# Four row blocks instead of six in the first phase of a two-layer graph kernel, a seven-product output projection, and an earlier place for a row of scores

## The chip, the cores and the metric

The kernel runs on one core of one Trainium2 chip. The metric is the device time of one execution in microseconds (us), lower is better. The time before is a median of three runs. A profile of one more execution shows what each engine did: TensorE (PE; its weight loads are listed as PEld), VectorE (DVE), ScalarE (ACT), GpSimd (POOL) and SyncE (SP, which only issues DMAs here).

## The reference

Two layers over a sparse graph with N = 4096 nodes and F = 512 features, all in fp32. `adj` is 4096 x 4096, some 0.8% of it nonzero, symmetric in its pattern. Cut to what is computed:

```python
h = relu(layernorm(x))                        # layer 0
d = rowsum(adj) ** -0.5
x = x + relu((d[:, None] * adj * d[None, :]) @ h @ W0 + b0)

h = relu(layernorm(x))                        # layer 1, attention
Wh1, Wh2 = h @ W1 @ a[:F], h @ W1 @ a[F:]
e = leaky_relu(Wh1 + Wh2.T, 0.2)
att = softmax(where(adj > 0, e, -1e12), axis=1)
neg = -softmax(where(adj > 0, -e, -1e12), axis=1)
x = x + elu(concat([att @ h, neg @ h], axis=1) @ wtrans)
```

Layer 0 multiplies by all of `adj`; layer 1 needs only the rows of `h` at the nonzero places of `adj`.

## The kernel before, in words

The nodes are cut into 32 blocks of 128 rows, called tiles here. A matmul of two fp32 operands appears in the profile as two records, and each has its own weight load. [...] an accumulator holds its bank from its first matmul until another engine has read it.

**First phase.** A loop over the 32 row blocks j loads x[j] (POOL's queue), normalizes and transposes it (`turn_x`), projects it with W0 (`project`, L679), and loads the four quarters of adj[j] (SP's queue, nine buffers) whose sums on ACT and DVE give d[j]. `scale` (L702) evicts the projection as y0[j]. In the same loop the tiles of the first entry of `GROUPS`, six of them (26 to 31), are accumulated directly: `load_at` fetches the block of the transposed adjacency `adj_t` (SP's queue, five buffers), `multiply` (L852) does one product of 128 x 512 per tile into one bank each, and `pack` turns the block into a mask of bytes (DVE here) and writes it to tables in DRAM on POOL's queue.

**Groups.** The other 26 tiles go in seven groups, the rest of `GROUPS`: six of four tiles and, last, (24, 2). The function `group` walks over 16 pairs of row blocks jp. Two tiles times two row blocks are a 2 x 2 block product, which is done by seven products of 128 x 256 instead of eight (`multiply_blocks`, L893). It uses sums of blocks of `adj_t` (`sum_at`, L880 to L883, DVE, three buffers named sums) and sums of y0 (`sum_y`, made in the first such group). A tile of `at` covers 8 // n row blocks, so one load, and one set of sums, serves one jp in a group of four and two jps in a group of two. While a group multiplies, the group before it is finished: `join_blocks` (or `evict` for the first phase's accumulators) combines the products on DVE, and `finish0` adds bias and residual, normalizes into h on ACT (two buffers h), computes two dot products with h on DVE (L816), writes x1, and puts h in eight tables, one copy on POOL's queue and seven on ACT's. In each step `finish0` of one tile is called. `EARLY` names groups whose masks are made early, by the index b of the group in which that happens. From b = 3 and b = 5 on, lists of the nonzero places are made on DVE, piece by piece in each step (`listing`, L391 and L393), and joined by POOL's DMAs.

**Between the layers.** In the last group gathering for layer 1 starts. The memory is cut into pools that are stacked from the left, and others from the right: `late_mask` and `late` (late_h, ut0, s_pair) lie on the right. A pool that lies over an earlier one waits for the last reader of that memory.

**Layer 1.** `sparse_layer1` handles half tiles r of 64 rows, two to a tile, in the order `order`; the tile of `PAIR0` was done ahead. For each tile POOL issues 22 indirect gathers of 128 rows (L451) in three parts into six buffers; even r use the first two parts, odd r the last two. `weights` makes scores (L463), leaky relu (L469), both exponentials (ACT, L473), masks (L482), and sums by a tree (L487 to L493), two half tiles ahead of the product. `product` does 14 accumulating products (L1296, 28 records), a matmul `cs` for the sums, and an eviction with the inverse sums on ACT (L1305). `turn` transposes the result into ut on PE and ACT (L508, L512). After each odd r but the first, `finish1` does the output projection of a tile by eight products of 128 x 512 (L1319, 16 records) with wtrans in memory as wt_sb, applies elu and adds x1 (L1327 to L1331), and writes the tile. The rows of Wh1, the scores s, come by `load_s` (L1256) on SP's queue, in four-tile pieces.

The order on each engine is fixed when the program is built. The builder places instructions by its own estimate of when they are ready, starting from the order in the source; `tc.keep_in_program_order` exempts some. Once built, each engine works through its own list in order, and a wait holds up what stands behind it.

Of the kernel before, what the change touches and what calls it, by code (L numbers as in the profile page):

```python
# [20 lines left out]
IB = 512  # L21


GROUPS = ((26, 6), (16, 4), (20, 4), (0, 4), (4, 4), (8, 4), (12, 4), (24, 2))

EARLY = {(24, 2): (2,), (12, 4): (3,), (8, 4): (4,)}
PAIR0 = 16
Y_PARTS = (8, 11, 13)
T_PARTS = (7, 9)
# [230 lines left out]
def gcn_gat_kernel(  # L260
# [251 lines left out]
            nc.scalar.copy(ut[:, g, :, (r % 2) * RB : (r % 2 + 1) * RB], tp[:, :, g, :])  # L512


    late_mask = ctx.enter_context(sbuf(name="late_mask", bufs=1, side="right"))
    late_m = late_mask.tile([P, EJ, TT * P], U8, name="late_m")
    with sbuf(name="y0", bufs=1) as y_pool, sbuf(name="wa", bufs=1) as wa_pool, sbuf(name="bits", bufs=4) as bits_pool, sbuf(name="small0", bufs=4) as small, ExitStack() as rest, ExitStack() as lists:
        list_pool = lists.enter_context(sbuf(name="list", bufs=1, side="right"))
# [232 lines left out]
            nc.vector.scalar_tensor_tensor(y, acc, d_all[:, j : j + 1], b_bc, ALU.mult, ALU.add)  # L751
            return y

        def new_y(work, j, k):
            if k < 0:
                return work.tile([P, F], F32, tag="y", name=f"y{j}", bufs=4)
            if k == 0:
                spare.append(make_pool.tile([P, 3, F], F32, tag="keys", name="spare"))
            return spare[0][:, k]

        def evict(i0, acc, work, _):

            return {
                i0 + k: affine(new_y(work, i0 + k, k - 3), a, i0 + k) for k, a in enumerate(acc)
            }

        def join_blocks(i0, n, acc, work, new_w):

            ys = {}
            for x in range(n // 2):  # L770
                p16, p23, p45, p7 = acc[x]
                j0, j1 = i0 + x, i0 + n // 2 + x
                ys[j0], ys[j1] = y, v = [new_y(work, j, -1) for j in (j0, j1)]
                w = new_w(f"w{j0}")[:, :H]
                nc.vector.tensor_copy(y[:, :H], p16[:, :H])
                nc.vector.tensor_tensor(w, p16[:, H:], y[:, :H], ALU.add)  # L776
                nc.vector.tensor_tensor(y[:, H:], p45[:, H:], w, ALU.add)

                def first(p23=p23, y=y):
                    nc.vector.tensor_tensor(y, p23, y, ALU.add)  # L780

                def second(p7=p7, w=w, p45=p45, v=v):
                    two = "p (a f) -> p a f"
                    nc.vector.tensor_tensor(w, p7, w, ALU.add)
                    nc.vector.tensor_tensor(
                        v.rearrange(two, a=2),
                        p45.rearrange(two, a=2),
                        w.unsqueeze(1).to_broadcast([P, 2, H]),
                        ALU.add,
                    )  # L790
# [12 lines left out]
            return ys  # L803
# [178 lines left out]
                pack(bits6, i0, j, ats.pop(j), j < 2)  # L982
                mark()
        pending = (GROUPS[0], partial(evict, i0, acc))
        listing, joining, spare = [], [], []

        def make_lists(g):
            make_keys(g)
# [43 lines left out]
        def group(b, work, at_pool, sum_pool, step, prod, n_h=2):  # L1032

            nonlocal pending
            i0, n = GROUPS[b]
            nj = 8 // n
            (p0, pn), take = pending
            order = [p0 + k for k in ((0, 2, 1, 3) if b > 1 else range(pn))]
            ats, sums = {}, {}

            def prepare(jp):
                if 2 * jp % nj == 0:
                    ats[jp] = load_at(at_pool, i0, n, 2 * jp, nj)
                    sums[jp] = sum_at(sum_pool, ats[jp], n, f"sums{i0}_{jp}")
                else:
                    ats[jp], sums[jp] = ats[jp - 1], sums[jp - 1]
                if b == 1:
                    sum_y(jp)

            prepare(0)  # L1050
            for j in order[:2]:
                if j not in xrs:
                    load_xr(j)
            for jp in range(NP):
                if jp + 1 < NP:
                    prepare(jp + 1)
                mark()
                if jp == 0:
                    ys = take(work, prod)
                    p7 = bank(f"p7_{i0}")  # L1060
                    acc = [
                        [*(bank(f"p{k}_{i0 + x}") for k in (16, 23, 45)), p7[:, x * H : (x + 1) * H]]
                        for x in range(n // 2)
                    ]
                multiply_blocks(acc, n, jp, ats[jp], sums[jp])
                if (i0, n) not in EARLY:
                    pack(bits_pool, i0, 2 * jp, ats[jp])
# [23 lines left out]
        with sbuf(name="work0", bufs=2) as work, sbuf(name="sums", bufs=3) as sum_pool, sbuf(name="at", bufs=6) as at_pool:  # L1091

            def prod(name):
                return work.tile([P, F], F32, tag="q", name=name, bufs=1)

            for b in range(1, len(GROUPS) - 1):

                def step(jp):
                    if jp == 2 and b in (3, 5):
                        make_lists((1, 0)[b == 5])  # L1100
                    for _ in range((2, 3)[b == 6] if jp != 2 else 0):
                        if listing:
# [10 lines left out]
        late = ctx.enter_context(sbuf(name="late", bufs=1, side="right"))  # L1113
# [122 lines left out]
    def sparse_layer1():  # L1236
        with ExitStack() as pools:
# [5 lines left out]
            slots = ((0, 0), (1, 0), (1, 2), (1, 1), (0, 1), (0, 2))  # L1243
            g_pools = {s: pool("g%d%d" % s, 1) for s in slots}
            tmp, small, p_pool = pool("tmp", 1), pool("small1", 2), pool("p", 3)
            work, ut_pool, wt_pool = pool("work1", 2), pool("ut", 2), pool("wt", 1)
            warm = small.tile([P, 1], F32, tag="warm", name="warm", bufs=1)
            nc.scalar.activation(warm, sign, AF.Exp)
            wt_sb = wt_pool.tile([P, 2 * FC, F], F32, name="wt_sb")
            s_pool = pool("s", 2)  # L1250
            gath, wgt, us, uts, srow = {}, {}, {}, {PAIR0: ut0}, {}

            def load_s(k):

# [52 lines left out]
            def turn(r):  # L1307
                if r % 2 == 0:
                    uts[r // 2] = ut_pool.tile([P, 2, FC, P], F32, tag="ut", name=f"ut{r // 2}")
                turn_u(r, us.pop(r), uts[r // 2])  # L1310

            def finish1(j):
                ut = uts.pop(j)
                x1 = work.tile([P, F], F32, tag="x1", name=f"x1_{j}")
                nc.sync.dma_start(out=x1, in_=x1_dram[j])
                po = bank(f"o1_{j}")
                for g in range(2):
                    for c in range(FC):
# [4 lines left out]
                            start=g == 0 and c == 0,  # L1323
                            stop=g == 1 and c == FC - 1,
                        )
                e = work.tile([P, F], F32, tag="eo", name=f"eo{j}", bufs=1)
                nc.vector.tensor_scalar(e, po, 0.0, None, ALU.min)  # L1327
                nc.scalar.activation(e, e, AF.Exp)
                y = work.tile([P, F], F32, tag="y", name=f"y1_{j}", bufs=1)
                nc.vector.scalar_tensor_tensor(y, po, 0.0, x1, ALU.max, ALU.add)  # L1330
                nc.vector.scalar_tensor_tensor(e, e, -1.0, y, ALU.add, ALU.add)  # L1331
                nc.sync.dma_start(out=out[j * P : (j + 1) * P, :], in_=e)


            pairs = [(PAIR0 + n) % (NR // 2) for n in range(1, NR // 2)]
# [24 lines left out]
            for k, r in enumerate(order):  # L1360
# [8 lines left out]
                if k + 2 < len(order):  # L1369
                    weights(order[k + 2])  # L1370
                    if wanted and order[k + 2] % 8 == 7:
                        load_s(wanted.pop(0))
                if k:
                    turn(order[k - 1])
                if k == 2:
                    finish1(PAIR0)
                if k % 2 and k > 1:
                    finish1(order[k - 3] // 2)
            turn(order[-1])
            finish1(order[-1] // 2)  # L1380

# [41 lines left out]
```

## Time and profile before

| | us |
|---|---|
| runs | 2130.96, 2139.83, 2135.72 |
| median of the runs | 2135.72 |
| the profiled execution | 2098.72 |
| its span, first to last instruction | 2096.8 |
| PE busy | 1996.2 |
| DVE busy | 1120.1 |
| POOL busy | 917.0 |
| ACT busy | 511.3 |
| granted TensorE clock, mean | 0.981 |

The stages of the profiled execution, by PE's matmuls:

| stage | us from the span's start |
|---|---|
| first phase, L852 | 25.8 to 334.5 |
| group (16, 4) | 334.3 to 433.5 |
| group (20, 4) | 433.4 to 530.7 |
| group (0, 4) | 530.6 to 638.1 |
| group (4, 4) | 637.9 to 753.6 |
| group (8, 4) | 758.2 to 866.1 |
| group (12, 4) | 866.0 to 975.3 |
| group (24, 2) | 975.1 to 1030.6 |
| layer 1, L1296 | 1078.5 to 2073.4 |

An engine's busy time is how long its instructions ran; idle time counts only where the engine sets the end. In the rows of a timeline the first number is the start, the second the duration, and a bracket at the end tells how long the engine was idle before it and what ended that. In the rows of waits the numbers are total us, times, and the longest. All times in the profile belong to the one profiled execution, which was 37 us shorter than the median of the runs.

### The profile page before, as it was taken

To read this page: it belongs to the slowest core of one execution; us is meant where nothing else is said; L and a number is where in the kernel's file an instruction comes from. 1 tells how busy PE (TensorE), PEld (TensorE's weight loads), DVE (VectorE), ACT (ScalarE), POOL (GpSimd) and SP (SyncE) were. 2 spreads that over 40 slices of the span, in tenths; PEclk is the share of its full clock that TensorE was granted. 3 is DMA by queue.
4 is the path that set the end of the run, shared out by engine and by line. 5 is a ranking of instruction groups with operands and counts; after the bars stand their busy time and mean duration, and the time that the engine had idled before them with its cause. 6 is when DMAs were issued, how large, how long until landed. Compare 5 with 4: busy or idle time off the path is not lost.

```text
span 2096.8 us, 20037 instructions
## 1 busy us (share of the span) xinstructions
PE 1996.2 (95%) x6456; PEld 1180.1 (56%) x6456; DVE 1120.1 (53%) x2805; ACT 511.3 (24%) x876; POOL 917.0 (44%) x980
## 2 busy tenths in 40 slices
PE   7999999999899879899879999999999999999998
PEld 3444446888787768788634444444444444444443
DVE  5444436563798458945545455554544544445441
ACT  4645612222332310000111222212212211121120
POOL 2010001111113320220577777777777777776740
PEclk9999999999999999999989999999999999999999
DMA  9988927887887776383689888888888888888850
GB/s 381 366 307 321 371 71 252 290 284 220 307 281 256 253 222 238 90 270 111 204 265 302 255 288 293 263 287 254 271 240 274 261 258 245 242 247 236 240 161 22
DMA packets 188040, 524.11 MB, mean 250 GB/s; under 512 B 25235, under 2 KB 34419, under 8 KB 187926
## 3 DMA queue, kind: packets, MB, share of 16 engines
q0 software_dynamic: 71296, 275.22, 42.2%
q1 hardware_dynamic: 86640, 192.78, 27.1%
q10 hardware_dynamic: 29990, 54.75, 7.4%
q8 instruction: 52, 0.85, 0.2%
q14 instruction: 62, 0.51, 0.1%
HBM read 430.83 MB, written 102.92 MB: 255 GB/s over the span
## 4 chain that ended last, share of the span: by engine, by line
PE 49%; DVE 6%; DMA 5%; POOL 3%; issue 2%; ACTq 1%; ACT 0%; DVEq 0%; SPq 0%; POOLq 0%
PE u L1296 32%; PE o L1319 10%; PE p L893 5%; POOL g L451 3%; DMA g<-table,idx 2%; DVE keys L393 1%; PE tp L508 1%; DVE lst L391 1%; DMA table<-h 1%; DMA ld<-li,off 1%; DMA at<-in_adj_t 1%; PE u L1174 1%; ACTq L443 1%; DVE prod L816 0%; DMA table<-m 0%
## 5 line engine op out<-in xcount | busy, mean ns | idle before, releaser
L451 POOL DMA_INDIRECT g<-table,idx x704 | 747.8, 1062 | 259.9 <-issue 186.4
L1296 PE MATMUL u<-g,p 128*128 128x512 f32 x1736 | 762.4, 596 | 9.8 <-DVE p L482 9.8
L1296 PEld LDWEIGHTS u<-g,p 128*128 128x128 f32 x1736 | 326.0, 191 | 397.5 <-issue 362.9
L463 DVE TENSOR_TENSOR z<-g,s 128x512 f32<-128x512 f32 (+1 forms) x124 | 77.5, 625 | 390.4 <-DMA g<-table,idx 357.8
L893 PE MATMUL p<-t,sums 128*128 128x256 f32 x832 | 249.0, 384 | 13.3 <-DVE sums L881 13.3
L893 PE MATMUL p<-y,sums 128*128 128x256 f32 x832 | 252.0, 385 | 6.5 <-DVE sums L883 6.5
L893 PE MATMUL p<-y,at 128*128 128x256 f32 x832 | 252.4, 386 | 4.9 <-DMA at<-in_adj_t 4.6
L1319 PE MATMUL o<-wt_sb,ut 128*128 128x512 f32 x512 | 225.1, 592 | 0.5 <-ACT ut L512 0.5
L473 ACT ACTIVATE p<-z 128x896 f32<-128x896 f32 (+2 forms) x136 | 116.1, 905 | 268.3 <-DVE z L469 248.1
L893 PEld LDWEIGHTS p<-t,sums 128*128 128x128 f32 x832 | 159.6, 193 | 37.5 <-DVE sums L881 15.5
L893 PEld LDWEIGHTS p<-y,sums 128*128 128x128 f32 x832 | 160.7, 193 | 29.9 <-DVE sums L883 7.3
L852 PE MATMUL acc<-y,at 128*128 128x512 f32 x384 | 174.9, 593 | 2.4 <-ACT y L702 2.4
L482 DVE SCALAR_TENSOR_TENSOR p<-g,p 128x384 f32<-128x384 uint8 (+1 forms) x256 | 143.2, 620 | 63.3 <-ACT p L473 62.3
L893 PEld LDWEIGHTS p<-y,at 128*128 128x128 f32 x832 | 159.3, 193 | 30.7 <-ACT m L716 5.0
L727 POOL DMA_DIRECT2D table<-m x71 | 54.3, 766 | 248.5 <-ACT m L716 145.5
L1319 PEld LDWEIGHTS o<-wt_sb,ut 128*128 128x128 f32 x512 | 94.8, 190 | 107.8 <-issue 106.9
L716 ACT ACTIVATE m<-at 128x1024 uint8<-128x1024 f32 (+1 forms) x110 | 105.2, 987 | 183.8 <-DMA at<-in_adj_t 137.3
L893 PE MATMUL p<-t,at 128*128 128x256 f32 x416 | 126.3, 386 | 18.5 <-DVE w L776 17.7
L1305 ACT ACTIVATE us<-u,rl 128x512 f32<-128x512 f32 x62 | 42.5, 686 | 414.7 <-issue 217.4
L679 PE MATMUL yp<-w_sb,hx_t 128*128 128x512 f32 x256 | 123.2, 627 | 17.3 <-ACT y L702 14.8
L852 PEld LDWEIGHTS acc<-y,at 128*128 128x128 f32 x384 | 70.5, 190 | 80.5 <-issue 77.4
L413 POOL DMA_INDIRECT ld<-li,off x48 | 43.2, 901 | 159.8 <-DMA ld<-li,off 115.8
(182 smaller groups left out, 1718.5 us busy)
## 6 DMA issues: line engine op xcount, KB each, us to landing
at<-in_adj_t SPq DMA_DIRECT2D x136, 512.0 KB, 5.1
ar<-in_adj SPq DMA_DIRECT2D x128, 512.0 KB, 8.4
table<-h ACTq DMA_DIRECT2D x182, 258.0 KB, 5.8
table<-m POOLq DMA_DIRECT2D x55, 256.0 KB, 5.6
at<-in_adj_t SPq DMA_DIRECT2D x32, 384.0 KB, 5.0
g<-table,idx POOLq DMA_INDIRECT x704, 4.3
xr<-in_x SPq DMA_DIRECT2D x32, 256.0 KB, 3.5
x<-x1d SPq DMA_DIRECT2D x32, 256.0 KB, 5.2
```

The costliest lines, as they stand in the source:

```text
L413: return nc.gpsimd.indirect_dma_start(out=lst_dram[g][:, :], out_offset=bass.IndirectOffsetOnAxis(ap=off[g][:, e, c : c + 1], axis=0), in_ ...
L451: nc.gpsimd.indirect_dma_start(out=gt[:, k, :], out_offset=None, in_=table[2 * n // RPT], in_offset=bass.IndirectOffsetOnAxis(ap=idx[n // ...
L463: return nc.vector.tensor_tensor(z, t.to_broadcast([P, n, RB]), s.unsqueeze(1).to_broadcast([P, n, RB]), ALU.add)
L473: i = nc.scalar.activation(p[:, :, g, :], z, AF.Exp, scale=(1.0, -1.0)[g])
L482: nc.vector.scalar_tensor_tensor(e, m, 0.0, e, ALU.is_gt, ALU.mult)
L679: nc.tensor.matmul(yp, hx_t[j][:, c * P : (c + 1) * P], w0_sb[:, c, :], start=c == 0, stop=c == FC - 1,)
L716: nc.scalar.activation(m, at, AF.Sign)
L727: nc.gpsimd.dma_start(out=rows_of(t, e)[:, c:, ROW_W + (a - t * TT) * P // 4 : ROW_W + (b - t * TT) * P // 4], in_=masks[i0][:, c:, (a - i ...
L852: nc.tensor.matmul(a, at[:, 0, it * P : (it + 1) * P], y0[j], start=j == 0, stop=j == NJ - 1)
L893: i = nc.tensor.matmul(out, left[:, x * P : (x + 1) * P], right, start=jp == 0 and first, stop=jp == NP - 1 and (final or not first),)
L1296: nc.tensor.matmul(u, p[:, k0 + k].rearrange("p g c -> p (g c)"), gt[:, k, :F].bitcast(F32), start=k0 + k == 0, stop=k0 + k == nk - 1,)
L1319: nc.tensor.matmul(po, ut[:, g, c, :], wt_sb[:, g * FC + c, :], start=g == 0 and c == 0, stop=g == 1 and c == FC - 1,)
```

## The change

Three things change.

The first phase accumulates four tiles, (28, 4), instead of six. The two tiles left over become a group of their own, (26, 2), the third entry. The indices in `EARLY` and of the list work move by one with it, and in a group of two that is not early `pack` is called once for each load. `new_y` loses the extra buffers that the fifth and sixth accumulators were evicted into.

```diff
-GROUPS = ((26, 6), (16, 4), (20, 4), (0, 4), (4, 4), (8, 4), (12, 4), (24, 2))
+GROUPS = ((28, 4), (16, 4), (26, 2), (20, 4), (0, 4), (4, 4), (8, 4), (12, 4), (24, 2))
 
-EARLY = {(24, 2): (2,), (12, 4): (3,), (8, 4): (4,)}
+EARLY = {(24, 2): (3,), (12, 4): (4,), (8, 4): (5,)}
...
-            order = [p0 + k for k in ((0, 2, 1, 3) if b > 1 else range(pn))]
+            order = [p0 + k for k in ((0, 2, 1, 3) if b > 1 and pn == 4 else range(pn))]
...
-                if (i0, n) not in EARLY:
+                if (i0, n) not in EARLY and 2 * jp % nj == 0:
                     pack(bits_pool, i0, 2 * jp, ats[jp])
...
-                    if jp == 2 and b in (3, 5):
-                        make_lists((1, 0)[b == 5])
-                    for _ in range((2, 3)[b == 6] if jp != 2 else 0):
+                    if jp == 2 and b in (4, 6):
+                        make_lists((1, 0)[b == 6])
+                    for _ in range((2, 3)[b == 7] if jp != 2 else 0):
```

The output projection of layer 1 does 28 of its tiles in pairs, each pair by seven products of 128 x 256 for every quarter q. The sums of wtrans that this needs are made once, in four steps spread over four half tiles, partly in place; the memory for them and for the sums of ut (`blocks`) is what `late_mask` and `late` held, so these pools are closed first. The last two tiles and the first ones use `finish1` as before; wtrans' changed part is loaded once more ahead of the last two.

```diff
+            def ut_sums(n):
+
+                a, b = (chunks_of(uts[pairs[n + k]]) for k in range(2))
+                t = ts[n] = blocks.tile([P, 3, FC, P], F32, tag="t", name=f"ts{n}")
+                op = nc.vector.tensor_tensor
+                op(t[:, 2], a[:, :, 0], b[:, :, 0], ALU.subtract)
+                op(b[:, :, 0], b[:, :, 0], b[:, :, 1], ALU.add)
+                op(t[:, 1], b[:, :, 0], a[:, :, 0], ALU.subtract)
+                op(t[:, 0], a[:, :, 1], t[:, 1], ALU.subtract)
...
+            def finish_two(n):
...
+                x0, x1 = load_x1(j0), load_x1(j1)
+                p16, p23, p45, p7 = (bank(f"o{k}_{j0}") for k in (16, 23, 45, 7))
+                for q in range(FC):
+                    w, s = w_blocks[:, q], ws[:, :, q]
+                    for out_, left, right, first, last in (
+                        (p16[:, :H], a[:, q, 0], w[:, 0, :H], True, False),
+                        (p16[:, H:], t[:, 1, q], s[:, 0], False, True),
+                        (p45[:, :H], b[:, q, 1], s[:, 2], True, False),
+                        (p45[:, H:], b[:, q, 0], w[:, 0, H:], False, True),
+                        (p23[:, :H], a[:, q, 1], w[:, 1, :H], True, False),
+                        (p23[:, H:], t[:, 0, q], w[:, 1, H:], False, True),
+                        (p7[:, :H], t[:, 2, q], s[:, 1], True, True),
+                    ):
...
+                nc.vector.tensor_copy(y[:, :H], p16[:, :H])
+                op(c, p16[:, H:], y[:, :H], ALU.add)
+                op(y[:, H:], p45[:, H:], c, ALU.add)
+                op(c, p7[:, :H], c, ALU.add)
+                op(y, p23, y, ALU.add)
...
+                put_out(j0, y, y, x0)
+                put_out(j1, v, v, x1)
...
-                if k % 2 and k > 1:
-                    finish1(order[k - 3] // 2)
+                if odd and n >= 0 and not two:
+                    finish1(pairs[n])
+                if not odd and two and n % 2 == 0:
+                    ut_sums(n - 1)
+                if k == 3:
+                    lates.close()
+                    blocks = pool("blocks", 1)
+                    ws = blocks.tile([P, 3, FC, H], F32, name="ws")
+                    summing = w_sums()
+                if 3 <= k < 7:
+                    summing[k - 3]()
+                if k == len(order) - 2:
+                    nc.sync.dma_start(
+                        out=w_blocks[:, :, 0, H:],
+                        in_=wtrans.rearrange("(q k p) f -> p q k f", p=P, k=2)[:, :, 0, H:],
+                    )
```

`finish_two(n - 1)` is called after the product of an odd half tile and before `turn`, for every second tile. `put_out` is the end of `finish1` (minimum, exponential, maximum and residual, sum, write), now in a function of its own; its buffer eo is single, as before.

The pool of s in layer 1 is made before the pool of wt_sb, so that it lies where other memory lay before.

```diff
-            work, ut_pool, wt_pool = pool("work1", 2), pool("ut", 2), pool("wt", 1)
+            work, ut_pool, s_pool, wt_pool = pool("work1", 2), pool("ut", 2), pool("s", 2), pool("wt", 1)
...
-            s_pool = pool("s", 2)
```

More of the change, by code (lines that the diff above doesn't have):

```diff
@@ L512, in turn_u @@
             nc.scalar.copy(ut[:, g, :, (r % 2) * RB : (r % 2 + 1) * RB], tp[:, :, g, :])
-    late_mask = ctx.enter_context(sbuf(name="late_mask", bufs=1, side="right"))
+    lates = ctx.enter_context(ExitStack())
+    late_mask = lates.enter_context(sbuf(name="late_mask", bufs=1, side="right"))
     late_m = late_mask.tile([P, EJ, TT * P], U8, name="late_m")
@@ L752, in affine, with new_y @@
             return y
[L754 to L759, printed above, removed]
+        def new_y(work, j):
+            return work.tile([P, F], F32, tag="y", name=f"y{j}", bufs=4)
         def evict(i0, acc, work, _):
             return {
-                i0 + k: affine(new_y(work, i0 + k, k - 3), a, i0 + k) for k, a in enumerate(acc)
+                i0 + k: affine(new_y(work, i0 + k), a, i0 + k) for k, a in enumerate(acc)
             }
@@ L772, in join_blocks @@
                 j0, j1 = i0 + x, i0 + n // 2 + x
-                ys[j0], ys[j1] = y, v = [new_y(work, j, -1) for j in (j0, j1)]
+                ys[j0], ys[j1] = y, v = [new_y(work, j) for j in (j0, j1)]
                 w = new_w(f"w{j0}")[:, :H]
@@ L984, in gcn_gat_kernel @@
         pending = (GROUPS[0], partial(evict, i0, acc))
-        listing, joining, spare = [], [], []
+        listing, joining = [], []
         def make_lists(g):
@@ L1112, in gcn_gat_kernel @@
         lists.close()
-        late = ctx.enter_context(sbuf(name="late", bufs=1, side="right"))
+        late = lates.enter_context(sbuf(name="late", bufs=1, side="right"))
         late_h = late.tile([P, n_late, ROW_W], F32, name="late_h")
@@ L1249, in sparse_layer1 @@
             wt_sb = wt_pool.tile([P, 2 * FC, F], F32, name="wt_sb")
-            s_pool = pool("s", 2)
-            gath, wgt, us, uts, srow = {}, {}, {}, {PAIR0: ut0}, {}
+            gath, wgt, us, uts, srow, ts = {}, {}, {}, {PAIR0: ut0}, {}, {}
+            w_blocks = wt_sb.rearrange("p (q k) f -> p q k f", k=2)
+            H = F // 2
             def load_s(k):
@@ L1310, in turn, with load_x1 @@
                 turn_u(r, us.pop(r), uts[r // 2])
+            def load_x1(j):
+                x1 = work.tile([P, F], F32, tag="x1", name=f"x1_{j}")
+                nc.sync.dma_start(out=x1, in_=x1_dram[j])
+                return x1
             def finish1(j):
                 ut = uts.pop(j)
-                x1 = work.tile([P, F], F32, tag="x1", name=f"x1_{j}")
-                nc.sync.dma_start(out=x1, in_=x1_dram[j])
+                x1 = load_x1(j)
                 po = bank(f"o1_{j}")
@@ L1325, in finish1, with put_out @@
                         )
+                y = work.tile([P, F], F32, tag="y", name=f"y1_{j}", bufs=1)
+                put_out(j, po, y, x1)
+            def put_out(j, po, y, x1):
                 e = work.tile([P, F], F32, tag="eo", name=f"eo{j}", bufs=1)
@@ L1328, in finish1 @@
                 nc.scalar.activation(e, e, AF.Exp)
-                y = work.tile([P, F], F32, tag="y", name=f"y1_{j}", bufs=1)
                 nc.vector.scalar_tensor_tensor(y, po, 0.0, x1, ALU.max, ALU.add)
@@ L1332, in finish1, with w_sums @@
                 nc.sync.dma_start(out=out[j * P : (j + 1) * P, :], in_=e)
+            def w_sums():
+                w = w_blocks
+                return [
+                    partial(nc.vector.tensor_tensor, out, a, b, ALU.subtract)
+                    for out, a, b in (
+                        (ws[:, 1], w[:, :, 1, H:], w[:, :, 0, H:]),
+                        (w[:, :, 0, H:], w[:, :, 0, H:], w[:, :, 0, :H]),
+                        (ws[:, 0], w[:, :, 1, H:], w[:, :, 0, H:]),
+                        (ws[:, 2], w[:, :, 1, :H], ws[:, 0]),
+                    )
+                ]
@@ new lines, in chunks_of @@
+            def chunks_of(ut):
+                return ut.rearrange("p g (q k) i -> p (g q) k i", k=2)
+            def ut_sums(n):
[6 more added lines that the diff above has]
+                op(t[:, 0], a[:, :, 1], t[:, 1], ALU.subtract)
@@ new lines, in finish_two @@
+            def finish_two(n):
+                j0, j1 = pairs[n : n + 2]
+                a, b, t = chunks_of(uts.pop(j0)), chunks_of(uts.pop(j1)), ts.pop(n)
+                x0, x1 = load_x1(j0), load_x1(j1)
[11 more added lines that the diff above has]
+                    ):
+                        nc.tensor.matmul(
+                            out_,
+                            left,
+                            right,
+                            start=q == 0 and first,
+                            stop=q == FC - 1 and last,
+                        )
+                op = nc.vector.tensor_tensor
+                y = work.tile([P, F], F32, tag="y", name=f"y1_{j0}", bufs=1)
+                v = blocks.tile([P, F], F32, tag="v", name=f"y1_{j1}")
+                c = blocks.tile([P, H], F32, tag="c", name=f"c{j0}")
+                nc.vector.tensor_copy(y[:, :H], p16[:, :H])
[3 more added lines that the diff above has]
+                op(y, p23, y, ALU.add)
+                two = "p (a f) -> p a f"
+                op(
+                    v.rearrange(two, a=2),
+                    p45.rearrange(two, a=2),
+                    c.unsqueeze(1).to_broadcast([P, 2, H]),
+                    ALU.add,
+                )
+                put_out(j0, y, y, x0)
+                put_out(j1, v, v, x1)
@@ L1372, in sparse_layer1 @@
                         load_s(wanted.pop(0))
+                n, odd = (k - 2) // 2, k % 2
+                two = 0 < n < len(pairs) - 2
+                if odd and two and n % 2 == 0:
+                    finish_two(n - 1)
                 if k:
@@ L1376, in sparse_layer1 @@
                     finish1(PAIR0)
-                if k % 2 and k > 1:
-                    finish1(order[k - 3] // 2)
+                if odd and n >= 0 and not two:
[13 more added lines that the diff above has]
+                        in_=wtrans.rearrange("(q k p) f -> p q k f", p=P, k=2)[:, :, 0, H:],
+                    )
             turn(order[-1])
```

## The prediction

> **What bounds the kernel now.** I read the table of windows first, because the page's 95% for PE is a mean over stages. I cut the span at the stages' borders, found from the first and last matmuls of L852, L893 and L1296. Columns: window, us, then busy us of PE, PEld, DVE, ACT, POOL, then granted clock, DMA share, GB/s.
>
> ```profile
> 9.00:109.00 100.00, 91.43 (x238) 42.01 (x239) 50.69 (x164) 57.98 (x123) 19.99 (x37) 1.00 1.01 385
> 109.00:268.00 159.00, 146.09 (x371) 66.33 (x370) 71.96 (x213) 88.09 (x183) 15.35 (x24) 0.96 0.90 329
> 268.00:334.00 66.00, 66.00 (x170) 29.07 (x169) 23.27 (x60) 11.16 (x18) 2.39 (x5) 1.00 0.25 76
> 433.00:530.00 97.00, 97.00 (x451) 84.95 (x450) 50.12 (x141) 26.16 (x37) 15.30 (x26) 1.00 0.80 262
> 975.00:1030.00 55.00, 50.78 (x227) 43.28 (x225) 34.55 (x97) 8.89 (x14) 27.30 (x32) 0.97 0.79 249
> 1171.00:2082.00 911.00, 910.54 (x2377) 421.43 (x2377) 434.41 (x805) 184.80 (x314) 630.75 (x593) 1.00 0.79 244
> ```
>
> Rows one to three are the first phase: DMA is full at 385 GB/s for 100 us while PE has 9% idle; then the loads run out at 268 and PE works alone for 66 us. PE is the bound there, with DMA a close second. The last row, 43% of the span, is PE without a gap. So I went to PE's timeline for one period of it:
>
> ```profile
> 1525.82 7.03 PE L1319 MATMUL o<-wt_sb,ut 128*128 128x512 f32 x16
> 1532.69 0.28 PE L498 MATMUL cs<-ones,total 128*128 128x1 f32 x2
> 1532.83 12.26 PE L1296 MATMUL u<-g,p 128*128 128x512 f32 x28
> 1545.51 12.26 PE L1296 MATMUL u<-g,p 128*128 128x512 f32 x28
> 1558.05 7.03 PE L1319 MATMUL o<-wt_sb,ut 128*128 128x512 f32 x16
> ```
>
> Period 32.23 us for one tile; its output projection takes 1532.69 - 1525.82 = 6.87 us for 16 records, 0.429 each. Then what the other engines have to spare, from DVE's timeline and from POOL's waits in 1171 to 2082:
>
> ```profile
> 1549.55 1.14 DVE L487 TENSOR_TENSOR tree<-p 128x896 f32<-128x896 f32 x1
> 1554.19 0.69 DVE L463 TENSOR_TENSOR z<-g,s 128x512 f32<-128x512 f32 x1 [3.50 <-DMA g<-table,idx]
> 1561.88 0.56 DVE L463 TENSOR_TENSOR z<-g,s 128x384 f32<-128x384 f32 x1 [5.74 <-DMA g<-table,idx]
> ...
> POOL g L451 <- PE u L1296: 53.7, 43, 3.4
> ```
>
> DVE waits for gathers, but the p it finishes at 1549.5 feeds the product of 1577.74: 28 us of cover. POOL waits 53.7 us for PE's release of slots over some 26.4 tiles: 2.0 us a tile is all it has to spare.
>
> [...] after 3.86 us of idle at 975.7 the pairs of records at 980.71, 981.56, 982.41 start 0.85 apart, against 0.43 later. [...] a gather's issue takes 946 ns median and 1062 in the mean. [...] L1327 from PSUM takes 684 ns, L567 from SBUF, as wide, 419. [...] 385 was measured here, and I use that.
>
> **The parts.**
> *First phase.* Per row block j, L852 goes from 12 records to 8. Six take 2.58 us (111.80 to 114.38 in PE's timeline), so 4 x 0.43 = 1.72 us, x32 = 55.0 us of PE gone; the undisturbed step shrinks from 9.02 us (most starts of L852) to 7.30. It ran 25.8 to 334.5, 308.7 us, of which 32 x 9.02 less the missing last projection (3.8) = 285 is work and 24 stalls, half-rate clock after them included. DMA: a step now moves 2.10 MB of adj, 0.39 of adj_t, 0.26 of x, 0.10 of mask: 2.85 MB, at 385 GB/s 7.40 us, 82% of PE's step. After: 2.69 MB, 6.98 us, 96%. So the lead that the loads gain before 109 us builds up hardly at all, and late x (DVE waits 95.4 us for L433's x) hits PE more. In its favour: accumulators hold 4 of 8 PSUM banks, not 6, and 17.2 us of L679's and L852's gaps wait for ACT's y. I take 8 us more stalls: gain 47. Bounds: 66 (the waits for y go, some half-rate clock with them) and 30 (a step at the 350 GB/s of 9 to 268 takes 7.7 us, 13 us in all, plus 12 more stalls).
>
> *The group (26, 2).* It adds 16 x 7 x 2 = 224 records of L893. Pairs of them start 0.431 apart, so 48.3 us of PE, nothing beside it. The nearest row, (24, 2), took 55.5 (975.1 to 1030.6), with a gap of 3.86 and half-rate clock after it; (20, 4) took 97.4 of 97 ideal. DVE in it: 32 sums at 0.416 = 13.3, four finish0 of some 3.7 = 15, evictions 9, flags 5: 42 of 49 us. ACT's h waits for seven table copies and came every 9.7 us in the group at 433 (440.9, 450.4, 458.3, 470.0) without stalling PE, for three sums buffers cover 18 us of PE in both shapes. But here four tiles' finish0 fall in four half-size steps. I take 2.2 us stall: 50.5. Bounds 48.3 and 57. Its 4.2 MB of loads and 1 MB of masks left phase one. Lists, early masks and their groups only change index; three affine operations fewer before group one: nothing, PE had no gap there.
>
> *Projection by seven.* For two tiles 32 full records (13.74 us) become 56 half ones, 56 x 0.2155 = 12.07: 1.67 us gone, 14 times: 23.4. Weight loads of 190 ns fit under 215, as in L893. DVE per two tiles: four sums at 0.68, copy and three half adds 1.7, two full 1.36: 5.7 us more, 434 of 911 busy now, so hidden. The second put_out waits for the first's DMA (one eo buffer, 4.9 us to land); behind it on DVE stand the next scores, with 28 us of cover. The new wait is PE's for ut_sums: ready at the ut copy (1546.4 in the period shown), wanted at 1558: 11.6 us for 2.7 us of work. The w_sums are 4.4 us on DVE once, early, where it idles up to 7 us; the reload of wt has 25 us of products ahead of its use. POOL: DVE's two-input work is some 14.5 us a tile and stretches 22 gathers by 22 x 0.12 = 2.6; the edit adds 2.5 us, so 0.45. POOL's 30.2 becomes 30.7 against PE's 31.4: still behind PE. I take 1 us off for stray waits: gain 22.4. Bounds 24 and 7 (POOL's stretch four times as large).
>
> *s sooner.* The load of s was issued at 1064.61 behind memory in use, and PE idled 9.47 us before 1078.52. But the third product, at 1106.12, waited 0.35 us for p, whose gather POOL had issued back to back since 1049.76. The idle time moves in front of that product; gain 0.4, at most 3, at least 0.
>
> Sum: -47 + 50.5 - 22.4 - 0.4 = -19.3. The profiled execution took 2098.72 us (span 2096.8), so 2079.4. The runs shown have their median 37 us higher, 2135.72, which this profile doesn't explain; I carry the difference over: 2116.
>
> **Rivals.**
> A, phase one runs free: the step is 7.30, the y waits vanish, gain 60, the group costs 49, projection 23.4: -35, 2101. For it: banks and the 66 us of PE alone; against: DMA at 96%.
> B, DMA or POOL takes the gain: phase one gains 35 with the group at 51, and the projection 15 as POOL tightens: +1, 2137. For it: 385 GB/s and 2.0 us of POOL slack; against: the loads can lead through five adj_t buffers.
> C, slower: ut_sums stand behind the gather waits in DVE's fixed order. Behind the second (1561.88) they end near 1565.8, and finish_two at 1557.6 starts 8 us late, 14 times: +115, less 19, 2231. It decides from (19.3 + 10.7) / 14 = 2.1 us per pair of tiles. Against: they are ready before those waits begin.
> D, the sooner s does nothing: within 0.4 us of my forecast, part of every case.
>
> **How the numbers follow.** Forecast (with D) 0.50, A 0.17, B 0.20, C 0.13. About 0.5%, 10.7 us, is what this measurement can tell from no change. Of the forecast's own spread (2105 to 2128) 0.07 lies within it; B gives 0.15 same, 0.03 faster, 0.02 slower. Faster 0.43 + 0.17 + 0.03 = 0.63, same 0.22, slower 0.15. Range 2095 to 2142: it leaves out C and A's best tail.
>
> **What would show it.** L852's last matmul near 287 (A: under 277; B: over 298). L893's first group starts there, and (26, 2) lasts about 50. Projection of two tiles near 12.1 us, the period of two tiles 62.8 instead of 64.5, and PE gapless after 1171. If PE waits for DVE's t in the projection, C is at work; if it waits for gathers, B. I am wrong if phase one ends after 317, or if the late stage keeps its 32.2.

## The result and the profile after

The change made the kernel slower. Over 15 runs each it took 2158.97 us in the median (2142.84 to 2177.17), before 2134.92 (2128.69 to 2144.67), a ratio of 1.0113 with a 95% interval of 1.009 to 1.0136. A ratio, here and below, leaves out executions over 1.5% longer than the fastest of their kernel (1 of 15 here, 15 of 22 for one kernel below), so it isn't quite the quotient of two medians. The forecast was 2116. The profiled execution of after took 2151.91 us, span 2150.1.

The six chips of the experiments below fall into two kinds, and half of the story hangs on that: on four the kernel before took 2130 to 2134 us (called the first kind here), on two 2101 (the second). None of them was used on two occasions, so whether it is the chip or something else about the occasion isn't told apart. The profiled execution of before that I forecast from (2098.72) looks like those of the second kind; the 15 runs of before and after look like the first.

The table of windows of after, cut at its stages. Columns as before: window, us, busy us of PE, PEld, DVE, ACT, POOL, granted clock, DMA share, GB/s.

```profile
26.00:109.00 83.00, 76.91 (x209) 35.22 (x210) 43.78 (x148) 53.58 (x114) 8.96 (x16) 1.00 0.98 370
109.00:273.00 164.00, 156.44 (x412) 69.40 (x410) 83.76 (x253) 94.53 (x194) 11.15 (x20) 1.00 0.85 316
...
371.00:427.00 56.00, 51.09 (x231) 44.12 (x230) 31.47 (x97) 12.48 (x19) 10.02 (x19) 0.97 0.88 285
...
1014.00:1026.00 12.00, 4.17 (x12) 1.92 (x10) 2.43 (x4) 3.27 (x4) 6.68 (x7) 0.72 0.78 242
1105.00:1145.00 40.00, 20.03 (x36) 8.49 (x36) 15.21 (x29) 4.34 (x10) 26.93 (x27) 0.67 0.88 290
1171.00:2100.00 929.00, 897.78 (x2686) 485.52 (x2685) 514.05 (x946) 183.99 (x305) 646.26 (x599) 0.99 0.77 239
```

The first phase ends at 272.8 instead of 334.5, sooner than I had forecast. But the last row is no longer PE without a gap: 31 us of it are idle, where before had 0.5 of 911. And in rows four and five, the last group and the head of layer 1, PE does 4 us of work in 12 and 20 in 40. PE's waits in after say what it idled for (us in all, times, longest):

```profile
PE u L1294 <- issue: 20.0, 17, 3.8
...
PE tp L508 <- issue: 16.2, 13, 4.5
PE cs L498 <- issue: 10.7, 11, 2.6
PE yp L680 <- DVE hx_t L655: 8.2, 5, 2.8
PE acc L849 <- ACT y L703: 7.9, 7, 2.4
```

"issue" is idle time in which the engine waited for no semaphore, so for no other engine and no transfer that the profile shows. It comes to 56 us here, 26 of them after 1165. The first profile of before has no such row. PE's timeline of one such stretch of after, behind an output projection (start, us, idle before in brackets):

```profile
1565.26 0.80 PE L1383 MATMUL o<-ws,ts 128*128 128x256 f32 x2
1566.41 0.31 PE L508 MATMUL tp<-ident,us 128*128 128x128 f32 x1 [0.35 <-issue]
1569.23 0.37 PE L508 MATMUL tp<-ident,us 128*128 128x128 f32 x1 [2.51 <-issue]
1571.38 0.37 PE L508 MATMUL tp<-ident,us 128*128 128x128 f32 x1 [1.78 <-issue]
1573.47 0.37 PE L508 MATMUL tp<-ident,us 128*128 128x128 f32 x1 [1.72 <-issue]
1574.87 0.40 PE L498 MATMUL cs<-ones,total 128*128 128x1 f32 x2 [1.03 <-issue]
```

The transposes need one `us`, which ACT had finished at 1554.5, yet they start 2.1 to 2.8 us apart. With their weight loads the starts lie at 1566.41, 1567.83, 1569.23, 1570.64, 1571.38, 1572.77, 1573.47: steps of 0.7 or 1.4 us. It looks as if PE got an instruction every 0.7 us or so; I call this a trickle. From 1568.9 to 1579.2 its granted clock is 0.5, and after 1165 the clock is halved for 30 us in all, in the first profile of before for 6. The cycle of two tiles, from one projection to the next, takes 63.4 us at best and 73.7 at worst, 66.6 in the mean of 13. The forecast had 62.8.

### The profile page after: what moved, and what is told of

Its sections match the earlier page's. It is cut to its first block, busy times and chain, and to the rows that moved or that the text cites. A ratio compares the mean times of both kernels' runs of the same rounds, so it can differ in the third digit from the quotient of the medians.

```text
span 2150.1 us, 21292 instructions
## 1 busy us (share of the span) xinstructions
PE 1992.7 (93%) x6890; PEld 1267.9 (59%) x6890; DVE 1212.4 (56%) x2995; ACT 520.8 (24%) x885; POOL 923.8 (43%) x980
## 4 chain that ended last, share of the span: by engine, by line
PE 47%; DVE 6%; issue 5%; POOL 4%; DMA 4%; another core or an unknown queue 1%; ACTq 1%; ACT 0%; DVEq 0%; POOLq 0%
PE u L1294 31%; PE o L1383 7%; PE p L890 5%; POOL g L451 4%; PE o L1321 1%; DVE keys L393 1%; PE tp L508 1%; DMA g<-table,idx 1%; DVE lst L391 1%; DMA ld<-li,off 1%; DMA table<-h 1%; DMA at<-in_adj_t 1%; ACTq L443 1%; PE u L1171 1%
## 5 line engine op out<-in xcount | busy, mean ns | idle before, releaser
L1294 PE MATMUL u<-g,p 128*128 128x512 f32 x1736 | 779.4, 605 | 28.3 <-issue 20.0
L890 PE MATMUL p<-t,sums 128*128 128x256 f32 x896 | 268.6, 384 | 20.3 <-DVE sums L878 16.7
L890 PE MATMUL p<-y,at 128*128 128x256 f32 x896 | 272.3, 386 | 9.5 <-DMA at<-in_adj_t 5.7
L890 PE MATMUL p<-y,sums 128*128 128x256 f32 x896 | 272.3, 386 | 2.7 <-DVE sums L880 2.1
L463 DVE TENSOR_TENSOR z<-g,s 128x512 f32<-128x512 f32 (+1 forms) x124 | 77.3, 624 | 267.9 <-DMA g<-table,idx 259.0
L890 PEld LDWEIGHTS p<-t,sums 128*128 128x128 f32 x896 | 172.0, 193 | 48.2 <-DVE sums L878 18.8
L890 PEld LDWEIGHTS p<-y,sums 128*128 128x128 f32 x896 | 173.6, 194 | 27.7 <-DVE sums L880 2.5
L890 PE MATMUL p<-t,at 128*128 128x256 f32 x448 | 136.2, 387 | 22.2 <-DVE w L773 21.3
L877 DVE TENSOR_TENSOR sums<-at 128x256 f32<-128x256 f32 x112 | 46.8, 417 | 174.8 <-PE p L890 122.7
L849 PE MATMUL acc<-y,at 128*128 128x512 f32 x256 | 120.9, 597 | 7.9 <-ACT y L703 7.9
L890 PEld LDWEIGHTS p<-t,at 128*128 128x128 f32 x448 | 85.8, 193 | 36.8 <-DVE w L773 22.9
L670 ACT ACTIVATE ar<-ar 128x1024 f32<-128x1024 f32 x96 | 100.2, 1044 | 10.5 <-DMA ar<-in_adj 10.0
L1303 ACT ACTIVATE us<-u,rl 128x512 f32<-128x512 f32 x62 | 42.4, 684 | 246.4 <-issue 142.6
```

What stands on the lines that cost most here:

```text
L463: return nc.vector.tensor_tensor(z, t.to_broadcast([P, n, RB]), s.unsqueeze(1).to_broadcast([P, n, RB]), ALU.add)
L670: i = nc.scalar.activation(ar, ar, AF.Identity, accum_out=part[:, c : c + 1])
L849: nc.tensor.matmul(a, at[:, 0, it * P : (it + 1) * P], y0[j], start=j == 0, stop=j == NJ - 1)
L890: i = nc.tensor.matmul(out, left[:, x * P : (x + 1) * P], right, start=jp == 0 and first, stop=jp == NP - 1 and (final or not first),)
L1294: nc.tensor.matmul(u, p[:, k0 + k].rearrange("p g c -> p (g c)"), gt[:, k, :F].bitcast(F32), start=k0 + k == 0, stop=k0 + k == nk - 1,)
```

## The experiments

Each was timed beside the kernel before on the same chip; "before" in this section is that one's median.

**One part at a time.** First the kernel before itself, then each part alone.

> The kernel before, unchanged, with a new profile. Theory 1 (the seven-product projection makes PE idle with no wait behind it): this profile has no idle of PE marked issue of more than 1 us in layer 1, as the first profile had none. Theory 3 (such idle times of PE belong to most executions, and the first profile of the kernel before, 37 us shorter than its runs, was one without them): here PE shows them too, some 30 to 40 us in all, and the time is near 2135.

Measured: 2135.0 us, ratio 1.0009 (0.9989 to 1.0029). Its profile has span 2133.0, 36 us more than the first profile. In the table of windows of this run:

```profile
1023.00:1033.00 10.00, 1.97 (x5) 1.23 (x5) 2.44 (x3) 3.28 (x4) 6.40 (x7) 0.71 0.85 262
1138.00:1164.00 26.00, 10.49 (x13) 3.24 (x12) 2.69 (x5) 0.00 (x0) 16.37 (x17) 0.60 0.79 249
1171.00:2100.00 929.00, 929.00 (x2427) 429.94 (x2426) 452.18 (x835) 188.96 (x318) 638.46 (x607) 1.00 0.80 245
```

Its waits by "issue" come to 32 us, all before 1165; the largest rows:

```profile
PE u L1296 <- issue: 12.7, 8, 4.4
PE p L893 <- issue: 8.2, 5, 2.4
```

So the kernel before has the same trickle, in the last group and at the head of layer 1, and none in the steady state. Here (24, 2) lasts 66.9 us instead of 55.5, and layer 1 ends 21 us later still: 32 of the 36 us between the two profiles. I had carried these over without knowing them.

```diff
-GROUPS = ((26, 6), (16, 4), (20, 4), (0, 4), (4, 4), (8, 4), (12, 4), (24, 2))
+GROUPS = ((28, 4), (16, 4), (26, 2), (20, 4), (0, 4), (4, 4), (8, 4), (12, 4), (24, 2))
```

> Only the first phase with four tiles and the group (26, 2). All theories: the first phase ends near 273 instead of 334, (26, 2) takes 50 to 55, so that group (0, 4) starts some 7 us earlier. Theory 1 and theory 2 (s lying elsewhere spoils the head of layer 1): the gain stays, 2128. Theory 3 allows anything from 2120 to 2145, as the idle times fall.

Measured: 2117.57 us, before 2133.16, ratio 0.9936 (0.9918 to 0.9954): a gain of 15.6 in the medians. In the windows of this run, and then of the run of before:

```profile
109.00:273.00 164.00, 157.74 (x413) 69.96 (x412) 84.86 (x254) 94.36 (x194) 11.15 (x20) 0.99 0.85 314
273.00:334.00 61.00, 60.13 (x276) 51.51 (x275) 46.18 (x137) 19.52 (x24) 9.98 (x19) 1.00 0.95 329
```

```profile
109.00:273.00 164.00, 151.71 (x387) 68.70 (x386) 74.44 (x221) 89.61 (x187) 15.34 (x24) 0.97 0.88 319
273.00:334.00 61.00, 61.00 (x154) 26.59 (x153) 21.32 (x52) 9.28 (x12) 2.38 (x5) 1.00 0.27 82
```

Before 273 PE idles 6 us instead of 12. After it, the 61 us in which before's PE works alone at 82 GB/s are filled by the next group's loads. The first phase is 60.3 us shorter (ends 273.9, not 334.2), the group (26, 2) costs 57.1, and (0, 4) is 11.2 shorter, 99.2 for 110.4, without its two waits of 2.82 and 4.20 us.

```diff
-                if k % 2 and k > 1:
-                    finish1(order[k - 3] // 2)
+                if odd and two and n % 2 == 0:
+                    finish_two(n - 1)
...
```

> Only the output projection by seven products. Theory 1: slower by 20 to 35 us, 2155 to 2170, with PE idle marked issue around the projections. Theory 2: faster by some 23 us, 2112. Theory 3: faster by up to 23 us, less where the idle times grow.

Measured: 2155.38 us, before 2133.16, ratio 1.0135 (1.0091 to 1.018), from six runs. This part alone turns the change into a loss. Its profile has 21.2 us of idle time by "issue" after 1165 and 40 us at half clock, where that of before has none and 5.

> Only the pool of s ahead of the pool of wt_sb. Theory 2: slower by about 20 us, 2155, lost between 1030 and 1150. Theory 1: no change, 2135 within 3 us. Theory 3: no change.

Measured: 2131.98 us, ratio 1.0003 (0.9985 to 1.0021): nothing, with only the line that makes `s_pool` moved.

**Dense records, or transfers?** The projection by seven issues 56 records and 56 weight loads in 12.1 us; it also loads x1 and writes the output of two tiles at once. Four kernels on the first phase of before were to tell these apart: the projection's eight products cut in halves; two tiles finished as a pair by eight products each; the projection by seven, mixed into the products of the next half tile; and the projection by seven with plain DMAs of consecutive rows instead of indirect gathers (it leaves out the gathering, so its output belongs to other rows).

```diff
+                        for h in (slice(0, F // 2), slice(F // 2, F)):
                             nc.tensor.matmul(
-                                po,
+                                po[:, h],
                                 ut[:, g, c, :],
-                                wt_sb[:, g * FC + c, :],
+                                wt_sb[:, g * FC + c, h],
```

> The kernel before; only each of the eight products of a tile's output projection is issued as two of 128x256 (32 records instead of 16 in the same 6.9 us, same operands, transfers and DVE work). Density theory (PE idles without a semaphore because so many short records, each with its weight load, come in a row while gathers run beside): idle time of this kind appears in the steady state after 1171 as in the kernel after; time 2145 to 2170. Transfer theory (two tiles' loads of x1 and outputs together, one eo buffer) and the theory of late sums on DVE: nothing changes, 2131 to 2141.

```diff
+                p0, p1 = bank(f"o0_{j0}"), bank(f"o1_{j0}")
+                for po, ut in ((p0, ut0_), (p1, ut1_)):
...
+                put_out(j0, p0, y, x0)
+                put_out(j1, p1, v, x1)
```

> The kernel before; the 28 tiles are finished two at a time at the places of the changed projection, with the same loads of x1 and the same outputs, but by eight products of 128x512 each and no sums. Density theory: no idle time without a semaphore in the steady state, 2130 to 2142. Transfer theory: as with the changed projection, which was 20 to 29 us slower and saved 22 in products, so 2170 to 2190 (up to 45 us over before). Late sums: no waits, 2130 to 2142.

```diff
                         nc.tensor.matmul(u, ...)
+                        for f in others[2 * (k0 + k) : 2 * (k0 + k) + 2]:
+                            f()
```

> Projection by seven alone, on the first phase of before, but the 28 products of two tiles are issued two after each of the 14 products of the next half tile, instead of in a row, so that no stretch has more than 6.2 records a us instead of 4.7 or 4.6. Density theory: the idle time without a semaphore goes or shrinks to a third; time 2110 to 2128. Transfer theory: still slower than before, 2145 to 2165. Late sums: the sums have 12 us more, so their waits go (about 6 us), 2140 to 2155.

```diff
-                gather(gt, n, a)
+                for x in range(CHUNKS[a]):
+                    nc.gpsimd.dma_start(out=gt[:, x, :], in_=table[2 * n // RPT][x * P : (x + 1) * P])
```

> Projection by seven alone, on the first phase of before, but in layer 1 each indirect gather is replaced by a plain DMA of 128 consecutive rows of the same table on the same queue, same bytes and slots, so scores, masks and output belong to other rows. Density theory where the gathers' part is essential: the idle time without a semaphore goes, also at the head of layer 1; 2070 to 2105, below the 2110 that the removed products promise. Density alone: it stays, 2135 to 2160.

These four fell on a chip of the second kind: before 2101.42 us. Measured 2101.62 (halves, ratio 1.0004), 2105.48 (pair, 1.0017, 1.0006 to 1.0027), 2095.86 (mixed, 0.9975, 0.9965 to 0.9985) and 2071.77 (plain DMAs, 0.9863, 0.9842 to 0.9883). None of the four profiles has idle time by "issue" after 1165, so they tell nothing on its cause. They tell the rest. The pair's transfers cost 4 us, not 20 to 29. In the mixed form, with indirect gathers and seven products, 11 of the 13 cycles of two tiles from 1197.8 on take 62.8 us here, as I had worked out. The first of the 13 takes 72.9, with waits of 6.21 us for `ts` and 1.99 for a sum on DVE, one takes 63.4.

**The whole change, the parts and dense records on one chip.**

> The whole change once more, beside a kernel before that is timed on the same chip. The runs so far fall in two sets: where before takes 2133 to 2135, PE idles without a semaphore; where it takes 2101, in the four experiments of the last call, it does not. Theory that the idle time is the chip's: if before takes about 2101 here, the change is a gain, my sum of -19 less some waits for DVE: 2080 to 2092; if before takes about 2134, it is 2150 to 2165. Theory that seven products lose by themselves: slower than before by 1% in both cases.

> Projection by seven alone. If before takes about 2101 here: 2080 to 2092 by the chip theory (23 saved, some 5 to 10 of waits for the sums of ut); if about 2134: 2148 to 2165 as measured. If seven products lose by themselves: slower than before in both.

> The whole change, with the 28 products of two tiles issued two after each product of the next half tile. If before takes about 2101: 2078 to 2092, about as the whole change. If about 2134: density theory 2100 to 2120 (the steady state without idle time), else 2145 to 2160.

> The kernel before with the products of layer 1 (p times gathered rows) and of its output projection each issued as two of 128x256: 9.3 records a us over the whole steady state, the same PE time, transfers and DVE work. If before takes about 2101: 2099 to 2112, no idle time without a semaphore, if the chip decides; 2150 or more if density alone decides. If before takes about 2134: 2200 or more by density, 2134 if not.

Before took 2129.89 us here, the first kind again. Measured: after 2158.11 (1.0107, 1.0071 to 1.0144); projection alone 2167.19 (1.0154, 1.0127 to 1.0181); the whole change in the mixed form 2163.01 (1.0067, 1.004 to 1.0094); all halves 2182.25 (1.023, 1.0208 to 1.0251). The mixed form's 22 runs spread from 2124 to 2192 us; its ratio rests on seven of them, whose median is 2145.19.

PE in one window of the profiles of projection alone and of the mixed form:

```profile
1171.00:2060.00 889.00, 852.73 (x2528) 458.60 (x2527) 486.94 (x894) 174.22 (x290) 626.43 (x586) 0.98 0.79 243
1171.00:2060.00 889.00, 840.33 (x2497) 453.13 (x2498) 477.79 (x889) 170.70 (x285) 625.21 (x582) 0.97 0.79 242
```

The last of the four settles that no new operand, sum or transfer is needed for a loss: the kernel before with all products of layer 1 cut in two, the same work for PE, loses 52 us here. On the second kind only the projection's products were cut, at no cost; all halves did not run there. PE's largest wait in the profile of all halves:

```profile
PE u L1297 <- issue: 39.6, 64, 1.8
```

Of these 39.6 us 21.9 come after 1165; the head of layer 1, where before has 12.7 of the kind, has the rest.

The mixed form is a miss for the density theory as I had put it. At 6.2 records a us in place of 9.3 the idle time stayed (42.4 us after 1165, in a profiled execution of 2161.38 us that isn't one of the seven; those seven still lose 0.7%). So the rate of records in a stretch doesn't decide alone. I then counted, in the traces of this kind of chip, the runs of gathers that POOL issues back to back (under 0.7 us between them). For those with idle time by "issue" of over 0.3 us, begun in the run or up to 1.5 us after its end, I counted PE's records and weight loads from the run's start to the first such idle time:

```
after 1165 us       runs  with idle   first idle: records in   us in
before              32    0           - (22 gathers: 152 to 160 in about 30 us)
after               34    10          161 to 274               23 to 44
projection alone    32    9           163 to 296               24 to 47
mixed form          27    11          140 to 340               24 to 56
all in halves       51    13          141 to 255               15 to 27
```

In nearly every such run the idle time lasts until about POOL's run ends, from 5 us before that to 3 us after. In halves it begins after 15 us, in the change after 23 or more, but in none of these 43 runs before 140 records; in 24 of them it begins between 140 and 190. That is no threshold: in after three runs of 22 gathers pass with 208 records and one of 36 gathers with 316, without idle time, and in the profile of the change's last repetition, at the end of this section, two begin after only 17 and 107 records. What can be said is that the projection by seven puts 24 records and loads more into each tile (112 for two tiles in place of 64), and that runs of gathers grow from 31 us at most to over 50. Why PE idles beside some runs of gathers and not beside others stays open.

Here are the first and the last rows of POOL's run in after that ends with the stretch shown above:

```profile
1531.68 1.11 POOL L451 DMA_INDIRECT g<-table,idx  x1 [2.16 <-PE u L1294]
1533.10 0.95 POOL L451 DMA_INDIRECT g<-table,idx  x1 [0.30 <-issue]
...
1569.96 1.23 POOL L451 DMA_INDIRECT g<-table,idx  x1 [0.31 <-issue]
1571.50 1.16 POOL L451 DMA_INDIRECT g<-table,idx  x1 [0.30 <-issue]
```

**Are the gathers needed?** Plain DMAs, the pair and the projection in halves once more, then plain DMAs and the whole change, for a chip of the first kind.

> Projection by seven alone, each indirect gather of layer 1 replaced by a plain DMA of 128 consecutive rows of the same table on the same queue (scores, masks and output belong to other rows), on a chip where PE idles without a semaphore if the draw gives one (before above 2125). Gathers essential: that idle time goes, at the head of layer 1 too, 2070 to 2100. Dense records alone: it stays, 2135 to 2165. If before takes about 2101 the run says nothing on this: 2072 again.

> Two tiles finished together by eight products of 128x512 each, no sums. If before is above 2125: density theory 2128 to 2142, no idle time without a semaphore after 1171; transfer theory 2150 to 2190. If before is about 2101: 2105 again.

> Only the eight products of each tile's output projection issued as two of 128x256 each: 32 dense records in 6.9 us where the change has 56 in 12.1. If before is above 2125: density theory 2145 to 2175, as all products in halves took 52 us more, a fifth of them in the projection; if only long bursts or the new operands matter, 2128 to 2140. If before is about 2101: 2101 again.

Again the second kind (before 2101.02): 2073.88, 2104.18 and 2103.59 us, each within 2.2 us of what it had taken. So the pair and the projection in halves were never timed on the first kind.

> Projection by seven alone with plain DMAs of consecutive rows in place of the indirect gathers (scores, masks and output belong to other rows). If before is above 2125 here: gathers essential, 2070 to 2100 and no idle time without a semaphore; dense records alone, 2135 to 2165. If before is about 2101: 2073 again, nothing on this.

> The whole change. If before is about 2101 here: 2076 to 2092, a gain, since the idle time that ate it does not stand on such a chip. If before is above 2125: 2150 to 2165 again. If seven products lose by themselves: slower than before by 1% in both cases.

Now the first kind: before 2134.03 us. The whole change took 2163.47 (1.01, 1.0074 to 1.0126). With plain DMAs the projection by seven took 2076.53 (0.9726, 0.97 to 0.9752), 3 to 5 us from its two times on the second kind: the difference between the chips is nearly gone. Its table of windows holds its own control, since the last group's gathers, for the tile done ahead, are still indirect in it:

```profile
1020.00:1033.00 13.00, 5.83 (x12) 2.97 (x12) 3.88 (x7) 3.27 (x4) 7.96 (x8) 0.65 0.79 233
1100.00:1160.00 60.00, 60.00 (x161) 28.09 (x160) 42.19 (x76) 15.17 (x27) 27.39 (x52) 1.00 0.96 373
1171.00:2060.00 889.00, 888.54 (x2716) 485.94 (x2715) 502.51 (x931) 184.01 (x310) 307.91 (x580) 1.00 0.70 244
```

Under indirect gathers PE trickles at 1020. Under plain DMAs it works 60 us of 60 at 373 GB/s, so it isn't the amount of traffic, and it works through all of the steady state. The cycles of two tiles are 62.8 us, 13 of 13 from 1197. The same kernel on the second kind of chip, in the window of the last group:

```profile
1020.00:1033.00 13.00, 13.00 (x61) 11.15 (x60) 5.69 (x12) 1.29 (x2) 10.25 (x10) 1.00 0.88 283
```

> The whole change. If before is about 2101 here: 2076 to 2092, since PE does not idle without a semaphore on such a chip; if seven products lost by themselves, above 2101. If before is above 2125: 2150 to 2165 once more, and what the change is worth on the other kind stays open.

The first kind again: before took 2131.98 us, the change 2147.77 (1.0082, 1.0054 to 1.0111). What the whole change is worth on the second kind was not measured, nor was the projection by seven in a row with indirect gathers; only its mixed form was, a gain of 0.25%.

## Why the prediction was wrong

*The step that failed* is "PE gapless after 1171", the path that the projection's term was added up on, with no cost for a PE that idles with work ready. It leaned on "Weight loads of 190 ns fit under 215, as in L893". The fit itself held: an undisturbed projection of two tiles lasted 12.1 us and the cycle 62.8, as the sum said, wherever PE did not trickle. But in the group that I had read for L893, at 433, no gathers run; in (24, 2), where L893 does run beside gathers, the one profile I had showed no trickle. Beside indirect gathers, on four of six chips, PE idled with work ready and then ran at half clock (granted 0.5, for 30 us after 1165 in after's profile): the term of -22.4 measured +22.2 us (2155.38 for 2133.16) and on another chip +37.3 (2167.19 for 2129.89). In after's profile that is a cycle of 66.6 us. What holds PE back stays open.

The parts account for the whole as well as can be measured. The ratios of the three alone, 0.9936, 1.0135 and 1.0003, come to 1.0073 together; the whole change measured 1.0082 to 1.0113 in four comparisons, with intervals that overlap.

*The 37 us* that the profile didn't explain I carried over as a constant. They were mostly the same idle time, in the last group and at layer 1's head; a difference of 1.8% between a profile and its runs was the sign that the profiled execution lacked something.

*First phase and (26, 2).* I had +3.5 us for both; the part alone measured -15.6. The first phase gained 61.7, near the 66 that I had as a bound and as rival A said: 55 us of work went as summed, and by the same sum (32 steps of 7.30 us less 3.8, in 246.2) the stalls fell from 24 us to 16 where I had added 8. PE's waits for ACT's y fell from 17.2 us to 7.9, with accumulators in four of the eight buffers of the pool `ps` instead of six, but didn't vanish, and the loads still came at 370 GB/s before 109. The group cost 55.4 to 57.1 for 50.5, through one gap of some 5 us, for the dot products and scores of the tiles being finished, that I hadn't placed; that is at or just over my bound of 57. The shorter (0, 4) I hadn't foreseen.

*s sooner*: nothing, as rival D said. *Rival C's* wait for ut's sums was real but rare: 3.05 us, once, in the profile of after. *Rival B*, 2137, came nearest in time, but not for its reason: after 1165 after's profile has no wait of PE for a gather or another transfer. PE did the same work in more time. No case of mine had an engine that idles with its work ready.

Of the versions that do the whole computation, the phase part alone has the best ratio, 0.9936 (2117.57 us): on a chip where PE trickles it beats both kernels. Pauses in the runs of gathers were not tried.

## What to carry to other kernels

A density of PE records that stands in one stage isn't always free in another (L893 kept PE busy for 97.0 of 97 us at 433; all products of layer 1 in halves lost 52 us on a chip of the first kind): look for a stage in the trace that has both the density and the company it will keep. Here (24, 2) was that stage, dense products under gathers, and on the first kind of chip it trickled (66.9 us instead of 55.5); only the one profile I had looked like the second kind. Idle time by "issue" on the bounding engine with work ready is a finding, not noise. And when the profile and the median differ by more than the change, find the difference first; time a candidate on more than one chip.

## What the runs showed of the hardware

Two kinds of chip: before took 2129.9 to 2134.0 us on four, with PE trickling under indirect gathers, and 2101.0 and 2101.4 on two, without it; the projection by seven with plain DMAs took 2076.5 on the first kind, 2071.8 and 2073.9 on the second. In the mixed form's trace of the second kind POOL issued gathers for 188 us from 1048 with no pause of 0.7 us, and PE had no idle time by "issue".

What PE waits for in a trickle, with its starts 0.7 or 1.4 us apart, is not shown. The trace of after has a queue of the kind "instruction" (q8) with 56 packets, 0.92 MB in all, each 0.9 to 1.4 us. They don't mark the idle times: of the 31 by "issue" of over 0.3 us after 1165, 3 overlap with such a packet. That the trickle comes from the gathers is an inference from the plain DMAs, and these differ in more than one way: POOL takes 0.54 us for each instead of 0.95 and up, issues eight in 4.2 us where eight indirect ones take some 10, and then waits for its buffers, so that its longest run after 1165 is 5.4 us, where the projection alone with indirect gathers has 50.7. Whether it is the indirect descriptors or the long runs of POOL isn't told apart.

A gather's own time shows DVE's work beside it. In the first profile of before, 210 gathers of the steady state with no DVE instruction beside them took 945 ns in the mean, none over 1 us; 382 beside DVE instructions took 1131. Not all of these count: 56 beside the scores (L463) alone, which have two inputs as well, took 945 too. That it is DVE's two-input work that stretches a gather was my estimate, from 946 ns in the median and 1062 in the mean; which of DVE's instructions do it is not shown.
